# New expected arrival times for the first loads in the planner of an attention and mixture-of-experts kernel

## The chip, the cores and the metric

The kernel runs on one core of a Trainium2 chip. The metric is the device time of one execution in microseconds (us); lower is better. Before the change it is 1156.06 us, the median of three runs (1155.9, 1156.06 and 1159.53).

Engines are named as the profile names them: PE is TensorE (PEld its weight loads), DVE is VectorE, ACT is ScalarE, POOL is GpSimd and SP is SyncE, which here only issues DMAs.

## What is computed

The input x has 4 sequences of 1024 tokens, each token 256 numbers, all float32. Two sandwiched layers follow one another; `_layernorm` stands ahead of and behind each.

```python
def linear_attn(q, k, v):                      # 4 heads of 64
    scale = DH ** (-0.25)
    q = jax.nn.softmax(q * scale, axis=-1)
    k = jax.nn.softmax(k * scale, axis=-2)     # over the tokens of a sequence
    context = jnp.einsum('bhnd,bhne->bhde', k, v)
    return jnp.einsum('bhnd,bhde->bhne', q, context)
...
h = layer_norm(x, ln1_g, ln1_b)
attn = linear_attn(h @ wq, h @ wk, h @ wv)     # split into heads and joined again
x = x + attn @ wo + bo
h = layer_norm(x, ln2_g, ln2_b)
x = x + jax.nn.gelu(h @ w_ff1 + b_ff1) @ w_ff2 + b_ff2
return x @ w_d + b_d
```

The second layer is a feed-forward block of 8 experts, of which each token uses two. The experts share w1, w3 and w2 and differ in low-rank additions (rank 16). The experts make up most of the time and aren't touched by this change.

## The kernel before

**Tiling.** The 4096 tokens are cut into 8 blocks of 512, two to a sequence. Each block is held as 128 partitions by 4 token tiles by 256. PSUM has eight banks of 128 x 512 float32.

**Streams.** The work is written as Python generators, so-called streams, that emit a few instructions and then yield. The streams in question here are:

- `front(i)` for each block i: loads z_i (for i above 1 inside the stream), takes its statistics on DVE (L300, L301, two token tiles at a time), makes 1/std (`rsqrt2`, L321 on DVE and the power on POOL, L324), normalizes z (L339 on DVE for token tiles 0 and 2, L345 on ACT for 1 and 3), transposes it on PE (`pt_h`, L288) and copies it out as hT (L490, ACT). Then come q (`pq` on PE, maximum and subtraction on DVE L506 and L508, Exp on ACT L512), k (`pk` on PE, maximum L525 on DVE, copy L526 and Exp L540 on ACT), the division of q (L560 to L562, DVE), the transposes `pt_q` and `pkt`, and `pz`, the product of k and z over the block's tokens (L596 for the first block of a sequence, L602 for the second, both on DVE). After the second block of a sequence there follow `pzk`, `pctx` and `pmix`, which turn the sums into one matrix for the sequence.
- `prepare_attn` (L367), once: `pv` and `pw` on PE, small products of a bias with wv and wo, and the scaling of wv (L389).
- `prepare_ff` (L392), once: 16 transposes of wff2 (`pwt`, four banks, copied out by ACT, L403), the product of wff2 and wd in four banks (`pwd`, copied out by DVE, L412), then `pbd`, `pcs` and `pbf` with their readers (L421, L426, L436), the scaling of wff1 (L439), and the fill of the DRAM table `rows` from a constant (L451).

**Who decides the order.** PE, DVE, ACT and POOL follow an order that the generators emit (`manual_schedule`). A planner inside the kernel keeps a modelled clock for each engine (`V`, `A`, `G`, and `pe` for PE) with a cost for each instruction. A stream says by the value that it yields when it can go on, and the planner steps the first stream that is ready, in the order closing, ready, tails, fronts, blocks, `first` (prepare_attn) and `once` (prepare_ff). A PSUM bank is picked as the one whose last reader ends earliest by the plan (`psum`). The dictionary `ARRIVE` (L368) tells the planner when the first loads will have landed; each stream yields the number of the load that it needs. These numbers set nothing on the chip: semaphores do the waiting, and a wrong number only places an instruction earlier or later in its engine's queue.

```python
# front
yield now() + 2.5 if i > 1 else ARRIVE[f"z{i}"]
# prepare_attn
yield ARRIVE["wqv"] + 1.0
# prepare_ff
yield ARRIVE["wff2"]
...
yield ARRIVE["wff1"]
```

**Loads.** SP and ACT issue them at the start: z_0 in halves on SP and ACT, then wq, wk, z_1, wv, wo, bo, and on SP wff2, wd, bd, wff1 and the weights of the experts, x_0 and x_1, then the fill of `rows`, then z_2 and z_3, which take the buffers of z_0 and z_1 and so wait until `pz` has read them.

Of the kernel before, what the change touches and what calls it, by code (L numbers as in the profile page):

```python
# [51 lines left out]
def sandwich_kernel(  # L52
# [143 lines left out]
    def now():  # L196
        return pe[0] / 2400.0 + idle[0]
# [69 lines left out]
    def small(shape, tag, name, bufs=None):  # L267
        return sm.tile(shape, F32, tag=tag, name=name, **({"bufs": bufs} if bufs else {}))
# [24 lines left out]
    def tiles(name, n=TB):  # L293
        return (small([P, n, 6], "st", f"st_{name}", 8),
                small([P, n, 2], f"mv{name[:2]}", f"mv_{name}", 6))
# [69 lines left out]
    cs_s = wp.tile([P, D], F32, tag="cs", name="cs")  # L365


    ARRIVE = {"z0": 4.5, "z1": 7.0, "wqv": 8.5, "wff2": 10.5, "wff1": 16.0}  # L368

    def prepare_attn():  # L370


        yield ARRIVE["wqv"] + 1.0
        bv = small([P, DC], "bv", "bv", 1)
# [20 lines left out]
    def prepare_ff():  # L395
        yield ARRIVE["wff2"]
        wff2T = mp1.tile([P, DC, FF], F32, tag="actB", name="wff2T")
# [30 lines left out]
        yield 0.0  # L428
        yield ARRIVE["wff1"]

# [30 lines left out]
    def front(i):  # L461
# [13 lines left out]
        z = zs[i]  # L475
        yield now() + 2.5 if i > 1 else ARRIVE[f"z{i}"]
        st, mv = tiles(f"in{i}")
# [1073 lines left out]
```

## Time and profile before

| | us |
|---|---|
| time, median of three runs | 1156.06 |
| the profiled execution's own time | 1165.82 |
| its span, first to last instruction | 1164.0 |
| PE matmul busy (94% of the span) | 1099.7 |
| PEld busy | 743.4 |
| DVE busy | 618.8 |
| POOL busy | 393.7 |
| ACT busy | 341.5 |
| DMA share, 2 to 52 us (slices of 2 us) | 0.92 to 1.12 |

The busy times add up instructions of each engine; PE works nearly all the time, and its granted clock is 0.981 of full speed on average. Its idle time lies at the start and in a few short gaps. The timeline of an engine lists its instructions in order of time, with the idle time ahead of a group in brackets and the engine or the DMA whose event ended it. A group's length runs from its first instruction's start to the modelled end of its last one, and matmuls are pipelined, so the next group can start some 0.2 us before that end.

### The profile page before, as it was taken

To read this page: it belongs to the slowest core of one execution; us is meant where nothing else is said; L and a number is where in the kernel's file an instruction comes from. 1 tells how busy PE (TensorE), PEld (TensorE's weight loads), DVE (VectorE), ACT (ScalarE), POOL (GpSimd) and SP (SyncE) were. 2 spreads that over 40 slices of the span, in tenths; PEclk is the share of its full clock that TensorE was granted. 3 is DMA by queue.
4 is the path that set the end of the run, shared out by engine and by line. 5 is a ranking of instruction groups with operands and counts; after the bars stand their busy time and mean duration, and the time that the engine had idled before them with its cause. 6 is when DMAs were issued, how large, how long until landed. Compare 5 with 4: busy or idle time off the path is not lost. (4 is left out here: it accounts for less than half of the span.)

```text
span 1164.0 us, 13016 instructions
## 1 busy us (share of the span) xinstructions
PE 1099.7 (94%) x4708; PEld 743.4 (64%) x4708; DVE 618.8 (53%) x1736; ACT 341.5 (29%) x684; POOL 393.7 (34%) x405
## 2 busy tenths in 40 slices
PE   5989998999999999999899999999999999999894
PEld 4867887766576677676576575766446766446342
DVE  4575656647637646736548647554343453443444
ACT  3335332513422542321342322221221221221321
POOL 1010022124223232423334313572452471642642
PEclk9989999999999999999999999999999999999997
DMA  9900002101100100000011000010000000100000
GB/s 320 222 18 29 9 19 74 56 1 37 37 1 19 56 19 19 28 10 19 24 41 47 17 3 19 20 38 1 12 26 1 10 29 1 37 0 1 19 1 20
DMA packets 26180, 39.50 MB, mean 34 GB/s; under 512 B 2432, under 2 KB 19712, under 8 KB 26112
## 3 DMA queue, kind: packets, MB, share of 16 engines
q1 hardware_dynamic: 21792, 28.68, 8.0%
q0 software_dynamic: 3072, 8.51, 2.0%
q10 hardware_dynamic: 1248, 1.44, 0.4%
q8 instruction: 39, 0.64, 0.2%
q14 instruction: 29, 0.24, 0.1%
HBM read 21.50 MB, written 17.12 MB: 33 GB/s over the span
## 5 line engine op out<-in xcount | busy, mean ns | idle before, releaser
L275 PE MATMUL ph<-tT,w_s 128*128 128x512 f32 (+1 forms) x640 | 234.9, 514 | 4.8 <-DVE act L1132 2.3
L275 PEld LDWEIGHTS ph<-tT,w_s 128*128 128x128 f32 x640 | 119.5, 191 | 97.2 <-issue 75.4
L275 PE MATMUL ph<-u,b_s 64*128 64x256 f32 (+2 forms) x512 | 164.4, 511 | 2.4 <-DVE act L1071 1.2
L275 PEld LDWEIGHTS ph<-u,b_s 64*128 64x128 f32 (+1 forms) x512 | 68.8, 189 | 83.9 <-issue 66.2
L275 PE MATMUL pf<-h2T,wff_s 128*128 128x256 f32 x512 | 117.1, 384 | 2.9 <-ACT h2T L687 2.5
L275 PE MATMUL py<-wff2d,g 128*128 128x256 f32 x512 | 115.7, 379 | 0.0
L275 PEld LDWEIGHTS pf<-h2T,wff_s 128*128 128x128 f32 x512 | 97.3, 192 | 19.3 <-ACT h2T L687 2.7
L1071 DVE SCALAR_TENSOR_TENSOR act<-act,ph 128x256 f32<-128x256 f32 (+1 forms) x96 | 48.6, 506 | 114.0 <-ACT act L1069 114.0
L275 PEld LDWEIGHTS py<-wff2d,g 128*128 128x128 f32 x512 | 97.3, 190 | 13.2
L1117 POOL TENSOR_TENSOR actB<-act,act 128x512 f32<-128x512 f32 x31 | 39.9, 1286 | 155.6 <-DVE act L1072 61.6
L1117 POOL TENSOR_TENSOR actA<-act,act 128x512 f32<-128x512 f32 x32 | 41.4, 1293 | 135.2 <-DVE act L1133 69.0
L707 ACT ACTIVATE g<-pf,bff 128x256 f32<-128x256 f32 x128 | 53.3, 472 | 103.2 <-PE pf L275 103.2
L1069 ACT ACTIVATE act<-ph 128x256 f32<-128x256 f32 (+1 forms) x96 | 40.3, 452 | 134.6 <-PE ph L275 105.0
L733 DVE SCALAR_TENSOR_TENSOR x<-py,std,x 128x256 f32<-128x256 f32 x32 | 15.5, 484 | 118.4 <-PE py L275 118.4
L275 PE MATMUL py<-u,b_s 64*128 64x512 f32 x128 | 67.0, 646 | 0.0
L275 PE MATMUL po<-w_s,actA 128*128 128x256 f32 x256 | 63.2, 386 | 0.6 <-POOL actA L1117 0.6
L1332 ACT COPY py<-ph 128x512 f32<-128x512 f32 x62 | 34.9, 569 | 93.5 <-PE ph L275 85.2
L275 PE MATMUL po<-w_s,actB 128*128 128x256 f32 x256 | 62.2, 382 | 0.0
L275 PEld LDWEIGHTS po<-w_s,actA 128*128 128x128 f32 x256 | 47.2, 191 | 20.3 <-issue 12.8
L890 POOL DMA_INDIRECT rows<-x,to x32 | 32.8, 1025 | 66.4 <-DVE x L856 19.4
L275 PEld LDWEIGHTS po<-w_s,actB 128*128 128x128 f32 x256 | 47.6, 190 | 11.9 <-issue 6.1
L1072 DVE TENSOR_TENSOR act<-act,ph 128x256 f32<-128x256 f32 (+1 forms) x96 | 48.9, 509 | 5.9 <-DVE act L1071 0.5
(246 smaller groups left out, 1775.1 us busy)
## 6 DMA issues: line engine op xcount, KB each, us to landing
rows<-none SPq DMA_DIRECT2D x1, 4208.0 KB
kept<-x SPq DMA_DIRECT2D x16, 263.0 KB
x<-in_x_dram SPq DMA_DIRECT2D x8, 512.0 KB, 5.7
row<-rows SPq DMA_DIRECT2D x6, 526.0 KB, 3.8
w_s<-in_w_dram SPq DMA_DIRECT2D x3, 1024.0 KB, 13.3
z<-in_x_dram SPq DMA_DIRECT2D x6, 512.0 KB, 3.4
wff_s<-in_wff_dram SPq DMA_DIRECT2D x2, 1024.0 KB, 10.7
row<-rows SPq DMA_DIRECT2D x4, 263.0 KB, 3.7
```

The costliest lines, as they stand in the source:

```text
L275: nc.tensor.matmul(out_, lhsT=lhsT, rhs=rhs, start=start, stop=stop, **kw)
L707: nc.scalar.activation(g[:, k * W : (k + 1) * W], pf[:, k * W : (k + 1) * W], AF.Gelu_apprx_tanh, bias=bff1_s[:, f : f + 1],)
L733: nc.vector.scalar_tensor_tensor(y[:, j, :], py[:, D : 2 * D], std[:, j : j + 1], y[:, j, :], ALU.mult, ALU.add)
L890: ins = nc.gpsimd.indirect_dma_start(out=dst[:, :], out_offset=bass.IndirectOffsetOnAxis(ap=at, axis=0), in_=src, in_offset=None, bounds_c ...
L1069: nc.scalar.activation(th, h1, AF.Tanh, scale=0.5)
L1071: nc.vector.scalar_tensor_tensor(th, th, 1.0, h1, ALU.add, ALU.mult)
L1072: nc.vector.tensor_tensor(th, th, h3, ALU.mult)
L1117: lambda x0=x0, x1=x1, op=op: nc.gpsimd.tensor_tensor(ac, x0, x1, op))
L1332: nc.scalar.copy(py[a], ph[a])
```

## The change

The five numbers of `ARRIVE` are replaced, nothing else:

```diff
-    ARRIVE = {"z0": 4.5, "z1": 7.0, "wqv": 8.5, "wff2": 10.5, "wff1": 16.0}
+    ARRIVE = {"z0": 4.3, "z1": 9.1, "wqv": 8.6, "wff2": 14.6, "wff1": 18.0}
```

Both kernels emit the same instructions on every engine. What differs is their order near the start. On PE it becomes (groups of matmuls and transposes; 0 and 1 are blocks):

```
before: pv, pwt x2, pt_h 0, pw, pwt x2, pq 0, pk 0, pt_h 1, pwd x2, pt_q 0, pkt 0,
        pq 1 (half), pz 0, pq 1 (half), pk 1, pwd x2, pbd, pcs, pbf, pt_q 1, pkt 1, pz 1
after:  pv, pt_h 0, pw, pq 0, pk 0, pwt x4, pt_h 1, pt_q 0, pkt 0, pwd,
        pq 1 (half), pz 0, pq 1 (half), pk 1, pwd x3, pbd, pcs, pbf, pt_q 1, pkt 1, pz 1
```

On DVE the normalization of z_0 moves ahead of the statistics of z_1, the normalization of z_1 moves behind the maximum of block 0's k, and the last two of the four copies of `pwd` change place with other work: the third stands ahead of block 1's division of q, and the fourth behind the first two statistics of z_2, where before all four stood ahead of them. On ACT the copies of `pwt` and the normalization of z_1 move behind the Exp of block 0's k. On POOL and SP the order stays; the bank in which `pz` of block 1 is summed is now the one that the fourth `pwd` used.

## The prediction

> **What bounds the kernel now.** I read the page first: PE is busy for 94% of the span, and section 4, the chain that ended last, covers only the last 1.7 us, so it says nothing of the stage that the change touches. The static order of the instructions of both kernels differs only in PE's rows 3 to 77, in DVE's up to the copy of pwd_6, and in ACT's up to row 24; behind the two kz instructions (L602) it is the same. That is the stretch from 0 to about 61 us of the trace, so I read its timeline engine by engine. PE first (columns: start, length, engine, line, operation, idle time before and who ended it):
>
> ```profile
> 9.33 1.83 PE L275 MATMUL pv<-vec,wqv_s 128*128 128x1 f32 x8 [9.33 <-DMA wqv_s<-in_wqv_dram]
> 14.42 1.94 PE L288 MATMUL pwt<-ident,wff_s 128*128 128x128 f32 x8 [3.26 <-DMA wff_s<-in_wff_dram]
> 16.16 1.91 PE L288 MATMUL pt_h<-ident,z 128*128 128x128 f32 x8
> 17.86 1.21 PE L275 MATMUL pw<-wo_s,bv 128*128 128x256 f32 x4
> 18.91 1.04 PE L288 MATMUL pwt<-ident,wff_s 128*128 128x128 f32 x8
> ...
> 51.76 1.40 PE L288 MATMUL pt_q<-ident,q 128*128 128x128 f32 x8
> 52.95 1.92 PE L288 MATMUL pkt<-ident,k 128*128 128x128 f32 x8
> 54.69 4.24 PE L275 MATMUL pz<-z,q 128*128 128x256 f32 x16
> 60.27 0.94 PE L288 MATMUL pzk<-ident,kz 128*128 128x128 f32 x4 [1.34 <-DVE kz L602]
> ```
>
> PE waits 3.26 us for wff2 with the first block's transposes queued behind it, and from 14.42 to 58.93 it has no gap. The next gap, 1.34 us at 60.27, is ended by DVE. So I read DVE next:
>
> ```profile
> 49.34 1.23 DVE L562 TENSOR_TENSOR q<-q,qsum 128x1024 f32<-128x1024 f32 x1
> 55.29 0.43 DVE L300 BATCH_NORM_STATS2 st_in<-z 128x6 f32<-128x256 f32 x1 [4.72 <-DMA z<-in_x_dram]
> ...
> 56.37 0.40 DVE L421 TENSOR_TENSOR bd_s<-bd_s,pbd 128x256 f32<-128x256 f32 x1
> ...
> 59.77 0.84 DVE L602 SCALAR_TENSOR_TENSOR kz<-kz,less,pz 128x256 f32<-128x256 f32 x2
> ```
>
> Here is the bound of this stage: DVE stands for 4.72 us until the third block's z has landed, and everything behind it to kz (59.77) runs without a gap. PE's dense stretch ends into that wait. The landing is a matter of the queue (SP's own timeline):
>
> ```profile
> 28.75 1.13 SPq L451 DMA_DIRECT2D rows<-none  x1
> 38.18 21.16 SPq L150 DMA_DIRECT2D z<-in_x_dram  x2
> ```
>
> The load of z_2 stands on SP's queue behind the 4208 KB fill of rows; the DMA share is 0.9 or more in every 2 us slice from 2 to 52 us, and at the fill's 190 to 250 GB/s it takes till about 53 us. z_2 can be issued as early as it likes: it lands at about 55.3.
>
> **The change, part by part.** It adds and removes no instruction and no DMA; the five numbers only reorder the plan.
>
> (1) *Start.* In the changed order z_0's normalization stands ahead of z_1's statistics on DVE (it now waits for rr_x at 7.78 instead of running at 11.18), and PE goes pv, pt_h of block 0, pw, pq, pk, then the four pwt. pv still waits for wqv at 9.33 and takes until about 11.1. z_0 is then ready (DVE 0.73, ACT 1.09 after 7.8: 9.1). So PE starts its dense work at 11.1 instead of 14.42: **3.3 us earlier**. hT is covered by pw: pt_h ends at 12.9 (1.74 us, as 14.42 to 16.16), the second hT at 13.8, pw at 14.6. Then pq 3.46 (19.78 to 23.24) and pk 3.43 (23.24 to 26.67) to 21.5, and four pwt at 0.87 per pair to 23.3; wff2 (landed at 14.4) is there.
>
> (2) *What is late next.* pt_h of block 1 needs z_1, and its normalization now stands on DVE behind kmax of the second pk, and on ACT behind the two Exp of k. In the trace that Exp chain ends 2.7 us after pk's last record (29.50 against 26.8); two normalizations on ACT take 1.09. That is about 25.4, and PE at 23.4 waits **1.9 us**. From there the rows add to 52.3 for the end of pkt of block 1, where before has 54.7 (pt_q, pkt, pwd, pq, pz, pq, pk, three pwd, pbd, pcs, pbf by the lengths of their rows). The front is about 1.4 to 2.4 us ahead there.
>
> (3) *Where it meets z_2.* In the changed order one of the four copies of pwd (L412) stands behind z_2's first two statistics on DVE, not ahead of them, so DVE's own work is done at about 47.4 and it waits until 55.29 all the same. The plan puts pz of block 1 into the bank of that very pwd, so pz has a wait on DVE that it did not have. The copy runs at 56.37 to 57.05 (0.69 as in its other rows). **pz of block 1 starts at 57.1 instead of 54.69**; PE stands from 52.3 to 57.1, 4.8 us. Nothing else is queued that could go first: PE takes its instructions in order, and pzk, pctx, pmix and pt_h of block 2 stand behind.
>
> (4) *From pz to pzk.* kz (L602) waits for all of pz. pz at full clock is 3.46 us (34.48 to 37.93 in the trace) and some 0.4 to the reader: kz at 60.95 against 59.77, **+1.2**. DVE's own chain would be ready at 59.77 + 0.66 = 60.43, so PE decides. But the clock will not be full. The granted clock by stretch (columns: stretch, length, busy time of PE, PEld, DVE, ACT, POOL, clock, DMA share, GB/s):
>
> ```profile
> 52.30:55.70 3.40, 3.40 (x15) 3.00 (x14) 0.41 (x1) 2.35 (x4) 0.00 (x0) 0.51 0.40 119
> 59.10:62.50 3.40, 1.50 (x9) 1.07 (x10) 1.52 (x7) 0.59 (x1) 1.01 (x1) 1.00 0.43 154
> 62.50:65.90 3.40, 2.76 (x10) 2.03 (x10) 2.40 (x10) 1.09 (x2) 0.00 (x0) 0.51 0.00 0
> 96.60:100.10 3.50, 1.50 (x10) 0.94 (x8) 1.18 (x4) 2.37 (x8) 0.00 (x0) 1.00 0.00 0
> 100.10:103.50 3.40, 2.90 (x7) 2.36 (x8) 3.25 (x13) 3.25 (x5) 0.00 (x0) 0.51 0.00 0
> ```
>
> Two stretches of 3.4 us in which PE was busy for only 1.50 us (59.10 and 96.60) are each followed by a stretch at half clock. A gap of 4.8 us surely brings that about. At half clock a pass of pz takes 0.43 instead of 0.22 us, and the half clock lasts to the end of a stretch that is well filled: between about 1.3 us (if it falls well) and all of pz. If 3.4 us of pz run at half clock, that is 8 of its 16 passes, and it takes 1.7 us more: kz at 62.6, **+2.8**. All of pz at half clock: 6.9 us, kz at 64.3, **+4.5**. At full clock +1.2 stays. I take +3.1, a little above the middle, since 2.76 busy us (62.50) were followed by another stretch at half clock (the row at 65.90 has 0.50).
>
> (5) *Behind kz* the order is the same, pzk, pctx, pmix and pt_h wait for one another, and the whole shift goes through: 94% PE leaves nothing later that would take it up, and z_3, whose load waits for pz, lands 3.2 us after its issue and was used 6.1 us after it. In the trace these four ran at half clock from 62.5 to 69.4; behind a full pz some of them should find the full clock: pctx and part of pmix, 0 to 1 us given back. I take 0.5.
>
> **Sum:** 3.1 - 0.5 = +2.6 us, against the profiled execution's 1165.82 us (span 1164.0, 1.8 around it) 1168.4, and against the median 1156.06 of the three runs shown, 9.8 lower since nothing was recorded, **1158.7**. Bounds of the unknown clock: +0.2 (1.2 less 1.0) and +4.5.
>
> **The skill against the trace.** The trace halves the clock after a gap of 2.51 us (97.9 to 100.6) as well as after longer ones. The Trainium skill, "TensorE: Matmul & The Clock Gate", section "HAM oscillation — how this bites in real kernels", asks for no idle gap of PE above about 3.4 us, which this change breaks at 52.3; by it pz would start at half clock too, and only the 1.9 us gap at 23.4 would surely be free, where the row leaves it open. The eight transposes of pwt took 1.94 us at 14.42 and 1.04 at 18.91, with transposes and four passes of pw between them. The same page's Part 4 says that transposes do not count as activity for the clock; by it block 0's pq would run at half clock till some 18 us, 1.7 us lost at the start, which the wait for z_2 would swallow, so the sum is the same; by the row they do count.
>
> **The rivals.**
> - *pz of block 1 all at half clock, slower.* Place: PE at 57.1. Price +4.5, less 0 to 1 given back: 1159.6 to 1160.6. It decides once more than about 5 us from 57.1 on are at half clock, that is when the boundary of the clock's stretches falls soon after 57.1 and the first part-filled stretch does not count. For: the row at 62.50. Against: the best-filled stretches (52.30) lift the clock after one.
> - *The gain is kept, faster.* z_2 lands before DVE needs it, because its load, issued at about 35 instead of 38.18, is taken ahead of the fill's end. Then pz follows pkt at 52.3 or so and all is 1.4 to 2.4 us earlier, at most the 3.3 of the start: 1152.8 to 1154.7. Against: the DMA share is full to 52 us and the load was issued 17 us before it landed.
> - *It doesn't do what it says.* Then block 0's chain would still wait for wff2. The order shows that it doesn't, so I give this no more than a share in the error of the others.
>
> **How the numbers follow.** Forecast (the wait for z_2 eats the gain, and pz's bank adds 0.2 to 3.4): 0.54. Half clock throughout pz: 0.33. Gain kept: 0.13, of it 0.05 beyond the bound. What a measurement here can tell from no change is about 0.3%, 3.47 us: slower means above 1159.5, faster below 1152.6. So faster 0.05, same 0.54 + 0.08 = 0.62, slower 0.33. The range leaves out the top of the second case and most of the third: 1154.6 to 1161.0.
>
> **What would show it.** Right: PE's pwt comes behind pk; pt_h of block 0 at about 11; a PE gap of 1 to 2.5 us ahead of pt_h of block 1, ended by ACT; DVE's wait for z_2 is about 8 us and still ends near 55.3; PE has a gap of some 4 to 5 us ahead of pz that ends with a copy of L412 near 57; pzk begins at 61.5 to 65. Wrong: z_2's statistics before 52, or pz without a gap, or pzk at or before 60.3.

## The result and the profile after

| | before | after |
|---|---|---|
| time, median of 20 runs each, us | 1160.01 (1155.29 to 1167.66) | 1164.95 (1161.43 to 1168.51) |
| ratio to before, 95% interval | | 1.0041 [1.0025, 1.0056] |
| the profiled execution: span, mean granted clock | 1164.0, 0.981 | 1163.0, 0.984 |

The change makes the kernel slower by 0.4%. The forecast was 0.2%, called "the same". Beware of the last row: of the two profiled executions the slower kernel's is the shorter one. This is explained below.

PE's timeline of the changed kernel (start, length, engine, line, operation, idle time before and who ended it):

```profile
11.14 1.95 PE L288 MATMUL pt_h<-ident,z 128*128 128x128 f32 x8
12.88 1.91 PE L275 MATMUL pw<-wo_s,bv 128*128 128x256 f32 x4
14.59 4.70 PE L275 MATMUL pq<-wqv_s,hT 128*128 128x256 f32 x16
...
26.03 1.26 PE L288 MATMUL pt_h<-ident,z 128*128 128x128 f32 x7 [1.45 <-ACT z L345]
...
47.88 4.06 PE L275 MATMUL pbf<-vec,wff_s 128*128 128x1 f32 x32
51.80 1.95 PE L288 MATMUL pt_q<-ident,q 128*128 128x128 f32 x8
53.54 1.92 PE L288 MATMUL pkt<-ident,k 128*128 128x128 f32 x8
57.48 5.50 PE L275 MATMUL pz<-z,q 128*128 128x256 f32 x16 [2.02 <-DVE wff2d L412]
63.55 0.94 PE L288 MATMUL pzk<-ident,kz 128*128 128x128 f32 x4 [0.57 <-DVE kz L602]
...
77.10 7.07 PE L275 MATMUL pa<-mix,qT 128*128 128x256 f32 x32
```

The first block's transposes start at 11.14, where PE before began its dense work at 14.42: 3.28 us earlier. Most of that is gone by 47.88, where `pbf` starts; before it started at 48.27. Then `pbf`, `pt_q` and `pkt` are slow, and `pz` of block 1 waits for a copy of `pwd` on DVE (L412), although it does not read that copy: it only takes over the PSUM bank. DVE's timeline shows why the copy is late:

```profile
55.58 0.43 DVE L300 BATCH_NORM_STATS2 st_in<-z 128x6 f32<-128x256 f32 x1 [7.14 <-DMA z<-in_x_dram]
...
56.67 0.66 DVE L412 COPY wff2d<-pwd 128x512 f32<-128x512 f32 x1
57.25 0.41 DVE L421 TENSOR_TENSOR bd_s<-bd_s,pbd 128x256 f32<-128x256 f32 x1
...
63.01 0.87 DVE L602 SCALAR_TENSOR_TENSOR kz<-kz,less,pz 128x256 f32<-128x256 f32 x2 [2.28 <-PE pz L275]
```

z_2 landed at 55.58, where it landed at 55.29 before, and DVE stood for it for 7.14 us instead of 4.72. The copy is queued behind z_2's statistics. In before DVE ran without a gap from z_2's statistics to `kz`; now it waits 2.28 us for `pz`, so PE has become the later of the two. From z_2's statistics to `kz` it takes 63.01 - 55.58 = 7.43 us, before 59.77 - 55.29 = 4.48 us.

The changed kernel's granted clock in this stage (stretch, length, busy time of PE, PEld, DVE, ACT, POOL, clock, DMA share, GB/s):

```profile
48.90:52.30 3.40, 3.40 (x27) 3.40 (x27) 0.00 (x0) 0.00 (x0) 0.00 (x0) 0.79 1.08 221
52.30:55.70 3.40, 3.15 (x15) 2.75 (x13) 0.12 (x1) 1.97 (x4) 0.00 (x0) 0.50 0.35 130
55.70:59.10 3.40, 1.62 (x4) 1.39 (x5) 3.33 (x10) 0.37 (x1) 0.00 (x0) 0.50 0.02 5
59.10:62.50 3.40, 3.40 (x12) 2.80 (x12) 1.57 (x7) 0.00 (x0) 0.00 (x0) 0.70 0.00 0
62.50:65.90 3.40, 2.09 (x13) 1.26 (x12) 0.95 (x3) 0.59 (x1) 1.01 (x1) 1.00 0.42 154
```

The clock was halved from 50.9, some 4.6 us ahead of PE's gap (`pkt` ends at 55.46), to 61.1: three stretches of 3.4 us. `pz` runs through the last of them, so it takes 5.50 us where 3.62 is its length at full clock. Behind 61.1 the clock is full; before, it was half from 62.6 to 69.4. So the changed kernel gets something back behind `kz`: from `kz` to `pa` of block 0, by which the clock is full in both, it takes 77.10 - 63.01 = 14.09 us. In before `pa` started at 75.55, so there it is 75.55 - 59.77 = 15.78.

**Why the profiled pair points the wrong way.** I matched PE's matmuls of the two executions by their number and followed the difference of their starts. At `pa` the changed kernel is 1.55 us late and stays 1.5 to 1.9 us late until 290 us. Before's execution has half-clock stretches at 298.1 and 560.9 that the other does not have; at each the difference falls by about 1.65 us. At the end the changed kernel is 1.1 us early. Such stretches lie all over the span: in before at 100.1, 188.9, 298.1, 560.9, 653.1 and 1090.0, in after at 102.1, 190.9, 651.7 and 1088.6. With all half-clock time taken out (each such microsecond counted as half), the changed kernel is 1.55 us late at `pa` and 2.3 us late at the end: most of its loss arises ahead of `pa`. Which of them an execution has differs from one to the next.

To take this out, I use each execution's span times its mean granted clock: that is the span it would have had at full clock, if all of the work followed PE's clock. It varies by about 1 us (standard deviation) within a kernel of the table below, where before's times vary by more than 10 us from lowest to highest and by 3.5 to 4.1 us in standard deviation. In the twenty first runs of the changed kernel it varies by 1.8 us. It does not take out the slow start: the clock's record begins where the clock is first full, 14 to 18 us into the span, and what ran slowly ahead of that is seen only in the lengths of its rows. The half-clock time is twice the span times (1 - clock).

### The profile page after: what moved, and what is told of

Its sections match the earlier page's. It is cut to its first block, busy times and chain, and to the rows that moved or that the text cites. A ratio compares the mean times of both kernels' runs of the same rounds, so it can differ in the third digit from the quotient of the medians.

```text
span 1163.0 us, 13017 instructions
## 1 busy us (share of the span) xinstructions
PE 1098.1 (94%) x4708; PEld 742.8 (64%) x4708; DVE 619.3 (53%) x1736; ACT 341.1 (29%) x684; POOL 393.6 (34%) x405
```

## The experiments

The kernels of one table group ran on the same chip and share its runs of before. "Full-clock span" and "half clock" are means over all timed executions, as just defined.

| kernel | ratio to before, 95% interval | full-clock span, us | half clock, us |
|---|---|---|---|
| before, group 1 (median 1164.49, 28 runs) | | 1144.9 | 37.1 |
| e1_act_copy | 1.0000 [0.9977, 1.0024] | 1143.7 | 40.8 |
| e2_before_bank | 1.0018 [0.9998, 1.0038] | 1146.6 | 36.9 |
| e5_after_fill | 0.9935 [0.9909, 0.9961] | 1143.1 | 26.8 |
| e6_before_fill | 0.9949 [0.9927, 0.9970] | 1144.0 | 27.8 |
| before, group 2 (median 1164.20, 29 runs) | | 1144.7 | 36.2 |
| r_before | 1.0002 [0.9980, 1.0025] | 1144.8 | 37.8 |
| r_after | 1.0025 [1.0001, 1.0049] | 1147.4 | 36.5 |
| e3_after_z2 | 0.9917 [0.9885, 0.9950] | 1140.0 | 28.9 |
| e7_wff2_fill | 0.9945 [0.9921, 0.9970] | 1142.7 | 28.5 |
| before, group 3 (median 1166.19, 15 runs) | | 1144.7 | 37.4 |
| e4_before_z2 | 0.9925 [0.9895, 0.9956] | 1141.1 | 26.3 |
| e8_wff2_z2 | 0.9914 [0.9883, 0.9946] | 1140.1 | 27.7 |

The main theory is the prediction's: DVE's wait for z_2 swallows the earlier start, and `pz`, tied by its bank to a copy behind z_2's statistics, makes the stage longer. The rivals are that the new order of the front costs time by itself, wherever z_2 lands, and that only the half clock's place or amount differs.

**The copy away from DVE** (e1_act_copy). The changed kernel, but ACT makes the fourth copy, so that `pz` does not wait for z_2:

```diff
-            nc.vector.tensor_copy(
+            (nc.scalar.copy if f == FC - 2 else nc.vector.tensor_copy)(
```

> The changed kernel, but the fourth copy of pwd is made by ACT, which is idle from 44 to 52.9 us, and no longer by DVE behind z_2's first statistics, so pz of block 1 finds its bank free. Theory 1 (the loss is pz's bank, whose reader stands behind the landing of z_2): PE's gap ahead of pz shrinks from 2.0 us to a few tenths, pz starts at about 55.6 instead of 57.5, kz is bound by DVE again at about 60, pzk at 60.3 to 61.5 instead of 63.55; time within 0.2% of before, 3 to 4 us under the changed kernel. Theory 2 (the new order of the front itself is what costs: a longer start at half clock and the wait for z_1): pz starts earlier but the time stays 0.4% above before. Theory 3 (the difference arises later, from where the stretches of half clock fall): pzk moves, the end doesn't.

Measured: 1.0000 [0.9977, 1.0024]. At full clock this kernel is 1.2 us shorter than before, and it has 3.7 us more of half clock, worth half of that; r_after below, the changed kernel without this edit, is 2.7 us longer than before at full clock. PE's timeline of this kernel:

```profile
51.82 3.72 PE L275 MATMUL pz<-z,q 128*128 128x256 f32 x16 [0.34 <-ACT q L583]
62.23 1.29 PE L288 MATMUL pzk<-ident,kz 128*128 128x128 f32 x4 [6.69 <-DVE kz L602]
```

`pz` runs ahead of the landing (57.24 here), and DVE's chain from z_2 to `kz` takes 61.73 - 57.24 = 4.49 us as before. In this execution the front's lead is still worth nothing: PE now waits 6.69 us for `kz`, and the clock was half from 58.3 to 72.0. The text for this run put `pz` at 55.6 and `pzk` at 60.3 to 61.5; they came at 51.82 and 62.23, since `pkt` ended sooner and z_2 landed later than in the first profile.

**The bank alone** (e2_before_bank). Before, but `pz` of block 1 is put by force into the bank that `pbd` used, whose reader (L421) stands behind z_2's first statistics; the rest of the order stays:

```diff
+    taken_by = {}
...
-        last[0] = slots.index(min(slots))
+        last[0] = taken_by["pbd"] if name == "pz_1" else slots.index(min(slots))
+        taken_by[name] = last[0]
```

> The kernel before, with one thing added: pz of block 1 is summed in the bank of pbd, whose reader (L421) stands behind z_2's first two statistics on DVE. The front is the old one. Theory 1: pz can't start before about 56.8 instead of 54.7, with a gap on PE ahead of it of about 2 us; kz at 61 to 63 instead of 59.8; time 2 to 4 us (0.2 to 0.35%) above before. Theory 2: the front is the old one, so the time is that of before within 0.1%.

Measured: 1.0018 [0.9998, 1.0038], which by itself does not exclude no change; the full-clock span is 1.7 us longer, some four times the standard error of that difference. Its PE timeline (lines are two higher than in before):

```profile
58.69 5.95 PE L277 MATMUL pz<-z,q 128*128 128x256 f32 x16 [5.55 <-DVE bd_s L423]
65.21 0.94 PE L290 MATMUL pzk<-ident,kz 128*128 128x128 f32 x4 [0.57 <-DVE kz L604]
```

The bank alone makes the picture of the changed kernel: a gap ahead of `pz`, a slow `pz` (the clock was half from 56.4 to 63.3), and 64.68 - 57.05 = 7.63 us from z_2's statistics to `kz` (the changed kernel 7.43). This speaks against the front's order as the cause.

**z_2 ahead of the fill** (e5_after_fill, e6_before_fill). In the changed kernel and in before, the fill of `rows` is issued in `front(2)` behind the loads of z_2 and z_3, so that z_2 does not queue behind 4208 KB:

```diff
+        G(0.6)
+        yield 0.0
+
+    def fill():
         none = mp2.tile([P, BLK], F32, tag="m0", name="none")
         nc.gpsimd.memset(none, float(NBLK * BLK))
-        G(0.6)
         nc.sync.dma_start(
...
-        yield 0.0
...
-        yield rsqrt2(mv, 1e-5, 1e-5, rr, f"x{i}")
+        rr_end = rsqrt2(mv, 1e-5, 1e-5, rr, f"x{i}")
+        if i == 2:
+            fill()
+        yield rr_end
```

> The changed kernel, with the fill of rows issued behind z_2 and z_3 instead of ahead of them; the order on PE, DVE and ACT is that of the changed kernel. z_2 then lands at about 41 to 44 and DVE doesn't wait for it. Theory 1: no gap ahead of pz; what is left of the front's gain shows, so this is 0 to 1.5 us faster than the next kernel (the one before with the same move), and 4 us or more faster than the changed kernel. Theory 2: it stays some 4 us slower than the next one.

> The kernel before, with the fill of rows issued behind z_2 and z_3. z_2 lands at about 41 to 44. Theory 1: DVE's 4.7 us wait goes, kz follows pz at 59.1 instead of 59.8, time 0 to 2 us below before. If the landing of z_2 mattered for neither kernel, the time is that of before.

Measured: 0.9935 [0.9909, 0.9961] and 0.9949 [0.9927, 0.9970]. DVE waits for no load here. Before gains some 6 us, where its text allowed 0 to 2; the last section comes back to this. PE's timeline of the changed kernel and then of before, each with the fill moved (lines from `front` on are five higher):

```profile
52.07 3.72 PE L275 MATMUL pz<-z,q 128*128 128x256 f32 x16 [0.34 <-ACT q L588]
56.37 0.94 PE L288 MATMUL pzk<-ident,kz 128*128 128x128 f32 x4 [0.57 <-DVE kz L607]
```

```profile
54.21 4.51 PE L275 MATMUL pz<-z,q 128*128 128x256 f32 x16
59.30 0.94 PE L288 MATMUL pzk<-ident,kz 128*128 128x128 f32 x4 [0.57 <-DVE kz L607]
```

In the changed kernel with the fill moved, `pz` starts at 52.07 and `pa` at 69.92, against 54.21 and 72.85. Not all of this lead is the order's: wqv landed 0.5 us sooner in the first execution, and the second has a half-clock stretch from 52.4 that the first has not, worth 1.7 us by `pa`. At the end of those two executions the lead was eaten again by half-clock stretches (five single ones behind 90 us against two). The means say it better: with the wait gone, the changed kernel's full-clock span is 0.9 us shorter than before's, where with the wait it is 2.7 us longer (below). So the front's order does not cost time by itself. The two intervals of the times overlap.

**Both kernels again** (r_before, r_after), unedited, for the spread and for a second look at the change.

> The kernel before, once more, for the spread between executions: where z_2 lands and which stretches run at half clock. Theory 1a (the forecast's sum was too small because the profile shown had two half-clock stretches behind kz, 62.5 to 69.4, that the kernel before usually doesn't have): kz again some 4.5 us after z_2's first statistics, and pa begins under 20 us after them, against 20.3 in the profile shown. Theory 1b (it is pz that usually runs at half clock from end to end in the changed kernel): pa again about 20 us after z_2.

> The changed kernel, once more, on the same chip as the run beside it. kz 7 to 9 us after z_2's first statistics (7.4 in the first profile), pz at half clock for most of its length. Theory 1a: much like the first profile, pa 21 to 22 us after z_2. Theory 1b: pz longer than its 5.5 us of the first profile, 6 to 7 us, pa 22 us or more after z_2. Time 0.25 to 0.55% above before.

Measured: 1.0002 [0.9980, 1.0025] and 1.0025 [1.0001, 1.0049]. At full clock the change costs 1147.4 - 1144.7 = 2.7 us, and the half-clock time is the same (36.5 and 36.2). So the amount of half clock is not the cause in this group. PE's timeline of before, run again:

```profile
53.47 3.80 PE L275 MATMUL pz<-z,q 128*128 128x256 f32 x16
62.70 1.29 PE L288 MATMUL pzk<-ident,kz 128*128 128x128 f32 x4 [5.43 <-DVE kz L602]
```

In this execution z_2 landed at 57.71, not at 55.29, and before itself has 5.43 us of idle PE here with 10.2 us of half clock from 60.5 on. In r_after z_2 came at 57.88 and `kz` 8.39 us later; PE's timeline, then DVE's:

```profile
14.51 3.62 PE L275 MATMUL pq<-wqv_s,hT 128*128 128x256 f32 x16
...
51.10 1.04 PE L288 MATMUL pkt<-ident,k 128*128 128x128 f32 x8
59.77 6.46 PE L275 MATMUL pz<-z,q 128*128 128x256 f32 x16 [7.63 <-DVE wff2d L412]
66.81 0.94 PE L288 MATMUL pzk<-ident,kz 128*128 128x128 f32 x4 [0.57 <-DVE kz L602]
```

```profile
57.88 0.43 DVE L300 BATCH_NORM_STATS2 st_in<-z 128x6 f32<-128x256 f32 x1 [10.62 <-DMA z<-in_x_dram]
...
66.27 0.87 DVE L602 SCALAR_TENSOR_TENSOR kz<-kz,less,pz 128x256 f32<-128x256 f32 x2 [3.24 <-PE pz L275]
```

Here the front ran at full clock from 14.2 on, `pkt` was done at 52.14, PE stood for 7.63 us, and the clock was half from 55.1 to 65.4, so nearly all of `pz` ran at half clock. The stage is as long as the landing makes it, and the landing varied from 55.3 to 57.9 in the six executions that issue the fill ahead of z_2 and have its statistics ahead of `kz`. The expectation that before has no half clock behind `kz` as a rule (1a) fell with these runs. That of a slow `pz` (1b) held in r_after: `pz` took 6.46 us, and `pa` started 22.5 us after z_2.

**The wait planned away** (e3_after_z2, e4_before_z2). Nothing is moved on SP; only the planner is told a late z_2, so that its statistics stand behind `kz` on DVE and block 0's `pa` goes first on PE. In the changed kernel, and with 52.0 in place of 54.0 in before:

```diff
-        yield now() + 2.5 if i > 1 else ARRIVE[f"z{i}"]
+        yield 54.0 if i == 2 else now() + 2.5 if i > 1 else ARRIVE[f"z{i}"]
```

> The changed kernel, with the plan told that z_2 lands late as well (54 instead of 2.5 us after its issue): z_2's statistics then stand on DVE behind all copies, scalings and kz, and block 0's pa goes ahead of block 2's transposes on PE. The load itself lands as late as before. Theory 1: no gap ahead of pz, kz follows pz at once (52 to 56), and the wait for z_2 is partly filled by pctx, pmix and pa; 3 to 7 us (0.25 to 0.6%) below before. Theory 2 (the order of the front is what costs): not below before.

> Before with one change: z_2 is planned at 52 us, so its statistics stand on DVE behind kz of block 1 and block 0's pa ahead of block 2's transposes; the fill of rows stays where it is. If the wait for z_2 is what the two kernels lose at this place, the ratio to before is 0.992 to 0.995, with about 27 us or less of half clock in the mean instead of 37, pz follows pkt without a gap, and z_2's statistics find z_2 landed. The changed kernel with the same edit stood at 0.9917; the front of the changed kernel starts 3.3 us earlier and gives back 1.45 to 1.7 us in front of block 1's transposes, so this one should be 0 to 1.6 us longer than that. Rival (the order of the front itself costs, whatever stands behind it): this one is shorter than the changed kernel with the same edit, 0.989 or less.

Measured: 0.9917 [0.9885, 0.9950] and 0.9925 [0.9895, 0.9956], on different chips. DVE's timeline of before with this one edit:

```profile
58.75 0.87 DVE L602 SCALAR_TENSOR_TENSOR kz<-kz,less,pz 128x256 f32<-128x256 f32 x2 [5.26 <-PE pz L275]
59.54 0.42 DVE L300 BATCH_NORM_STATS2 st_in<-z 128x6 f32<-128x256 f32 x1
```

The statistics find z_2 landed, and PE has no gap ahead of `pz`. The changed kernel gains 0.83% with this edit, more than its text allowed (0.25 to 0.6%). The full-clock span falls by 3.5 us in before and by 7.4 us in the changed kernel (against r_after); half-clock time falls by 11.1 and by 7.6 us, which is worth half of it. What the changed kernel lost to before (2.7) turns into 1.1 us of lead at full clock (1141.1 - 1140.0), as the text for e4 expected (0 to 1.6); the times, 1156.1 and 1155.0, do not tell the two apart. The rival, by which before with this edit is clearly the shorter one (0.989 or less), fell.

**One number of the five** (e7_wff2_fill, e8_wff2_z2). Before with only `wff2` set to 14.6, so that the first block's chain goes ahead of `pwt` but z_1's normalization is not put behind block 0's k; e7 with the fill moved, e8 with z_2 planned at 54:

```diff
-    ARRIVE = {"z0": 4.5, "z1": 7.0, "wqv": 8.5, "wff2": 10.5, "wff1": 16.0}
+    ARRIVE = {"z0": 4.5, "z1": 7.0, "wqv": 8.5, "wff2": 14.6, "wff1": 16.0}
```

> One part of the change alone, the late wff2 (14.6) with the other four old numbers, and the fill of rows behind z_2 and z_3. z_1 is then still planned early: its normalization isn't behind block 0's Exp, so pt_h of block 1 follows pk without a gap (1.45 us in the changed kernel), while z_0's normalization waits for z_1's statistics as in the kernel before (11.2 us), so PE's dense work begins at 12.2 instead of 11.1. Sum: 0 to 1 us below the changed kernel with the late fill, so about 0.6 to 0.75% below before. If the wait for z_1 were covered by other work anyway, it would be 1 us slower than that kernel.

> Before with one of the five numbers changed (wff2 14.6) and z_2 planned at 54: the first block's chain goes ahead of wff2, z_1's normalization is not behind block 0's k, and nothing waits for z_2. If the start's 3.3 us and the missing wait for z_1 go through once z_2 is not waited for, the span at full clock is some 1138.5 to 1140 us (1140.0 in the changed kernel with the same edit of z_2, 1144.8 before) and the ratio 0.989 to 0.992. Rival (what the front gains is lost at some later load or in half clock): the ratio is that of the changed kernel with z_2 planned late or higher, 0.992 to 0.995, with a new wait on a DMA in the first 60 us.

Measured: 0.9945 [0.9921, 0.9970] and 0.9914 [0.9883, 0.9946]. The start's gain is there (block 0's transposes at 10.80 and 11.54, where the text for e7 had 12.2) and block 1's transposes follow without a gap. But in both PE waits 1.13 us for the division of q (L562) ahead of `pt_q` of block 0: the missing wait for z_1 is replaced by another of nearly the same length. e8's full-clock span is 1140.1 us against e3's 1140.0. e7 is not ahead of e5 (0.9945 against 0.9935), though its text put it 0 to 1 us ahead. In e8 z_2 lands at 57.98 and DVE still waits 0.77 us, so 54 is a little early there; PE waits 0.4 us longer for it ahead of `pmix` than in e3 and as much less ahead of `pa`. All kernels in which nothing waits long for z_2 lie at 0.991 to 0.995 and beat both kernels of the case; the intervals do not rank them. At full clock those in which z_2 is planned late (1140.0 to 1141.1) are shorter than those with the fill moved (1142.7 to 1144.0). They also run block 0's `pa` ahead of block 2's transposes; whether that is the reason was not tried.

## Why the prediction was wrong

The mechanism was right, and the direction of the sum too; the base that the sum was added to was too low, and for the first measurement the sum was too small as well. Of the 6.25 us between the forecast of 1158.7 and the measured 1164.95, 3.95 lie in the base and 2.3 in the sum. The sum gave +2.6 us, 0.22%, and so "the same". The runs gave 0.41% [0.25, 0.56] and 0.25% [0.01, 0.49]; at full clock the second of these is 2.7 us.

1. *The start*, 3.3 us earlier: right (3.28), and in the order that was read off. But `pq` of block 0 took 4.70 us instead of the 3.46 that I put in, since some five of its 16 passes still ran at half clock: 1.1 us of the gain. I had worked out such a loss (1.7) only as an alternative and taken none, by the row at 14.42 of before. It depends on the execution: the full clock came 5.6 us after the first dense instruction here, 3.8 us after it in before, and 2.8 us after it in r_after, where `pq` took 3.62 us and nothing of this was lost.
2. *The wait for z_1*, 1.9 us ended by ACT: right in kind and size. One of the eight transposes went first, and the other seven waited 1.45 us. But with step 1's loss the front was 0.4 us ahead at `pbf`, not 1.4 to 2.4. And `pkt` ended at 55.5 instead of 52.3, since the clock was halved from 50.9; in r_after it ended at 52.14. This did not matter to the end, since z_2 swallows it.
3. *z_2 and the bank*: right. DVE's wait was 7.14 us (forecast about 8), it ended at 55.58 (55.3), the copy stood at 56.67 (56.37) and `pz` started at 57.48 (57.1). The gap ahead of `pz` was 2.02 us and not 4.8, because of the late `pkt`; in r_after, with a later z_2, it was 7.63.
4. *From pz to pzk*, taken as +3.1: measured from z_2's statistics to `kz`, 7.43 - 4.48 = +2.95 here, and 8.39 - 4.48 = +3.9 in the second pair. The size holds. The reason given does not hold in the profiled execution, where the clock had been half for 4.6 us when the gap began; there the size was luck. In r_after it does hold: the clock was full until 3.0 us into the gap and half from then on.
5. *Behind kz*, 0.5 us given back: measured 1.7 (14.09 against 15.78), and 2.1 in the second pair (14.10 against 16.24), since before's half clock falls there and the changed kernel's is over by then. I had put in `pctx` and part of `pmix`; `pmix`, `pt_h` and part of `pq` found the full clock too.

Steps 4 and 5 together give 1.25 to 1.8 us for one landing of z_2, less than the 2.6 forecast. With the half clock taken out, as the means count, the two pairs are 1.55 and 3.6 us apart at `pa`: in the second `pa` is 80.37 - 78.43 = 1.94 us later, and by then before has one half-clock stretch of 3.4 us more, worth 1.7. The 2.7 of the means lies between the two, so the sum of 2.6 has the right size for the second measurement. For the first, with 4.9 us between the medians, it is too small. Why that one is larger stays open: before's twenty runs of it have no clock on record, so their half-clock time can't be taken out. The changed kernel's twenty have 34.6 us of half clock and a full-clock span of 1146.0 us, 1.4 less than r_after's.

**The step that failed is the base**, the last term of the sum: 1156.06, the median of three runs, with the profiled execution's 9.8 us more put down to its being recorded. Before's 20 runs, the same three among them, have the median 1160.01, and the later groups 1164.2 to 1166.2. The profiled execution, at 1165.82, was an ordinary one, with 44 us of half clock (twice 1164.0 times 0.019); in every later run the profiled execution is one of the timed ones. The three runs were at the low end. With the right base the same sum gives 1162.6, and the range of 1154.6 to 1161.0, moved up by the same 3.95, ends at 1164.95, just where the measured median lies.

The second weak term is the price of `pz`'s new wait net of what is given back: 2.6 in the sum, 2.7 at full clock in the second measurement and 4.9 in the first. A sum of 2.6 lies just below the 3.47 us that I took for what a measurement can tell, and the case that came true, "slower", stood beside it at 0.33.

Of the rivals, "all of `pz` at half clock" named the right side; in the profiled execution it was not the event (`pz` took 5.50 us, not 6.9), and in r_after it nearly was (6.46). "The gain is kept" fell, since z_2 landed when it did before; e5 and e3 show that with z_2 out of the way some 1 us of it at full clock would have been kept.

**The gap and the clock.** In the changed kernel's profiled execution PE's longest gap in this stage was 2.02 us, and the clock had been halved 4.6 us before it. The Trainium skill, "TensorE: Matmul & The Clock Gate", section "HAM oscillation — how this bites in real kernels", asks for no idle gap of PE above about 3.4 us; here the clock fell with no gap at all, so keeping to that rule would not have kept it up. r_after, with half clock from 3.0 us into a gap of 7.63 us, agrees with it.

## What to carry to other kernels

An order that starts earlier is worth nothing if a later load ends the stage: find the wait that ends last there and move that one. Here one planned time for z_2 gave some 0.75%, and five times for earlier loads cost 0.25 to 0.4%. When an instruction is moved behind a wait, look at who takes over its PSUM bank, since that one waits too. And take the spread of the baseline from the granted clock of its executions before you trust the median of three runs to 1%.

## What the hardware showed

**The clock changes on a grid.** All half-clock stretches in the 12 profiles are multiples of 3.4 us long, except the one at the end of the span, and stand on one grid within an execution. The grid lies differently against each execution's start. A single stretch costs about 1.65 us (the difference of the first pair's starts fell from 1.88 to 0.23 at 298.1), and an execution of before has 25 to 47 us of half clock in all. This is most of the spread of its times: their standard deviation of 3.5 to 4.1 us falls to about 1 us when it is taken out.

**A matmul with one column seems to count as idle time.** `pbf` (32 matmuls of 128x1) keeps PE busy for 3.4 us or more without a gap. Set against the grid of each execution, the clock was halved right behind a stretch of which `pbf` filled 2.3, 2.7, 3.0, 3.0, 3.3, 3.4 or 3.4 us (seven executions), and not where it filled 2.0 to 2.1 us at most (the other five). The row of `pbf` above, with 3.40 busy us and a clock of 0.79 in the stretch from 48.90, is one of the seven. No run changed `pbf` itself, so this is a correlation, without an experiment.

**Waiting for one load cost twice here.** Where the wait for z_2 was taken away from before by moving the fill (e6), the full-clock span fell by 0.9 us only, but the half-clock time by 9 us, worth some 4.6 us. Together that is the 0.5% measured. Where it was planned away (e4), it was 3.5 us and 11.1 us of half clock, worth 5.5, together about the 0.75% measured.
